# A graph layer's second product: every block decoded from bytes, instead of four kept as ready weights

## The chip, the cores and the metric

The kernel runs on one core of one Trainium2 chip. A core has a matrix engine (TensorE, PE in the profile), a vector engine (VectorE, DVE), an activation engine (ScalarE, ACT), a general engine (GpSimd, POOL) and a sync engine that issues transfers (SyncE, SP). Each takes its own instructions in their order, and they wait for each other through semaphores. The metric is the time of one execution on the device in microseconds: the median of three runs.

## What is computed

Two graph layers over 3327 nodes of 64 features, with one adjacency matrix of 3327 x 3327. The first layer is a sum over pairs of nodes; the second is a product of a weight matrix with the features of all nodes. Cut to what matters:

```python
h = jnp.maximum(_layernorm(x, axis=-1), 0.0)
# layer 0, for all pairs (i, j)
adj_att = sigmoid(left[:, None] + right[None, :] + b_att[0]) * adj
x_local = logmap(x[:, None, :], x[None, :, :], c)
support_t = jnp.einsum('ij,ijd->id', adj_att, x_local)
x = x + proj(expmap(h, support_t, c), c)        # per node, over 64 features
# layer 1
h = jnp.maximum(_layernorm(x, axis=-1), 0.0)
support = h @ weight
mask = (adj != 0)
rank = jnp.cumsum(mask, axis=1)
deg = rank[:, -1:]
k = jnp.minimum(deg, 100.0)
pos = rank - (deg - k)
w = mask * jnp.where(pos > 0, 0.5 ** (k - pos), 0.0)
x = x + w @ support + bias
```

Each edge of the second layer has a weight that halves with every later edge of its row. It needs the same adjacency blocks as the first layer, so the kernel reads them once and keeps one number for each pair.

## The kernel before

The nodes are padded to 26 blocks of 128. The first layer goes over four strips of output nodes (8, 8, 6 and 4 blocks), and in each over the 26 source blocks j, from the last to the first, in rounds. A round loads a piece of the adjacency matrix (`ad`), makes a mask of it, lets PE count the later edges (`pc`), and keeps a byte for each pair (`behind`). Times 128 and read as a bf16 pattern, that number is the weight of the pair in the second layer, because it then stands in the exponent. The rest of a round is a tanh (`sg`), a product (`pq`), two Gelu, two vector instructions, and the product that sums over j (`po`).

```python
JD = range(12, 16)
AHEAD = 2
SGB, ADB = 5, 5
PORTIONS, LAST = (2, 4, 4, 8), 6
...
behind_hi = const.tile([P, NB - JD.stop, NP], U8, name="behind_hi")
weight_of = const.tile([P, len(JD), NP], U16, name="weight_of")
...
def read(n, j):                       # what is kept of a counted block
    kept = behind(j)[:, S.i0 : S.i0 + S.F]
    if (n < AHEAD and k == 0) or i * num // den != (i + 1) * num // den:
        A.activation(kept, S.pc[:, : S.F], AF.Relu, scale=128.0 if j in JD else 1.0)
    elif j in JD:
        V.tensor_scalar(kept, S.pc[:, : S.F], 0.0, 128.0, op0=ALU.max, op1=ALU.mult)
    else:
        V.tensor_scalar(kept, S.pc[:, : S.F], 0.0, None, op0=ALU.max)
```

Blocks 12 to 15 are kept as 16-bit weights (`weight_of`), ready for PE; the other 22 as bytes (`behind_lo`, `behind_hi`), to be decoded later.

When a strip's sums are complete, they are copied out (`strip_out`), transposed (`turn`) and go through the per-node work (`post`): products of 64 features on DVE, and chains of small steps on one number per node. For the first three strips the small steps run on POOL, hidden behind the next strip. For the last strip they run on DVE, with names ending in `_last`, and with each square root as a power on POOL:

```python
def root(y, v):
    power(y, v, nhalf)               # G.tensor_tensor(..., op=ALU.pow)
    mul(rt, y, y)
    ...
def post(agg, k):
    A.activation(u, v, AF.Square)
    V.tensor_mul(w, hs, v)
    ...                              # dots_last, of_sum_last, d_last, e_last, t_last; first root
    A.activation(k_, t0, AF.Tanh)    # k_last
    ...                              # e_last, of_end_last, d_last, y_last; second root
    V.tensor_add(xs, xs, u)
    V.tensor_reduce(t0, xs, AX.X, ALU.add)
    V.scalar_tensor_tensor(w, wide(t0, nb), -1.0 / D, xs, op0=ALU.mult, op1=ALU.add)
    A.activation(u, w, AF.Square)    # u_last<-w_last
    V.tensor_reduce(t0, u, AX.X, ALU.add)
    ...                              # third root
    V.scalar_tensor_tensor(w, w, 0.0, wide(rn, nb), op0=ALU.max, op1=ALU.mult)
    A.copy(s2[:, bs, 0], w)          # the cast
    V.tensor_sub(s2[:, bs, 1], w, s2[:, bs, 0])
```

The work is cut into portions, and `advance(n)` lets some of them into the order of instructions between others. In the second product the decodes alternate between ACT and DVE; each block is then multiplied with the features `s2`, in seven pieces. The four last blocks need the last strip's features and come at the end.

```python
weights = {j: decode(j) for j in order[: len(JD) + 1]}   # order: 12 to 15, then 0 to 11, then 16 to 21
stages.append(Stage(per_node(len(STRIPS) - 1, pa)))
...
def decode(j):
    if j in JD:
        return behind(j)
    wt = l1.tile([P, NP], U16, name="wt", bufs=7)
    decoded += 1
    if decoded % 2:
        A.activation(wt, behind(j), AF.Copy, scale=128.0)
    else:
        V.tensor_scalar(wt, behind(j), 128.0, None, op0=ALU.mult)
    return wt
...
for i, j in enumerate(order):
    if j not in weights:
        weights[j] = decode(j)
    asked_of_act()
    advance(LAST)
    for n in range(len(chunks)):
        add(j, weights[j], n)
finish()
for j in range(late, NB):            # blocks 22 to 25
    weights[j] = decode(j)
```

After that each of the seven pieces gets its last four matmuls, is copied, multiplied with the second layer's weight matrix, added to x and sent out. A check on the range of the values (`in_range`) sets a flag by which a slower general path would be taken; with these inputs it isn't.

Of the kernel before, what the change touches and what calls it, by code (L numbers as in the profile page):

```python
# [22 lines left out]
P = 128  # L23
# [4 lines left out]
K = D + 2  # L28
STRIPS = [(0, 8), (8, 8), (16, 6), (22, 4)]
FMAX = 8 * P  # L30
JD = range(12, 16)
IN_ORDER = {mybir.EngineType.PE, mybir.EngineType.DVE, mybir.EngineType.Activation}
AHEAD = 2
SGB, ADB = 5, 5
ON_ACT = ((1, 2), (5, 8), (3, 4), (1, 2))


PORTIONS, LAST = (2, 4, 4, 8), 6
BIG, LATER, ACT = 4, 99, 100
ROUND = (3.5, 3.5, 2.8, 1.9)  # L40

# [402 lines left out]
def fast(ctx, tc, x, adj_t, r, w_att, b_att, weight, bias, out, flag):  # L444
# [84 lines left out]

    jz = const.tile([P, NB, P], F16, name="jz")  # L530
    ju = const.tile([P, NB, P], F16, name="ju")
    behind_hi = const.tile([P, NB - JD.stop, NP], U8, name="behind_hi")
    weight_of = const.tile([P, len(JD), NP], U16, name="weight_of")
    s2 = const.tile([P, NB, 2, D], F16, name="s2")

    left_d = tc.dram_tile([NP], F32, name="left_d")
# [3 lines left out]
    behind_of = {}  # L540

    def behind(j):
        if j in JD:
            return weight_of[:, j - JD.start]
        return behind_of["lo"][:, j] if j < JD.start else behind_hi[:, j - JD.stop]

# [59 lines left out]
    def load(n):  # L608
        k, lo, hi = rounds[n]
        S = strips[k]  # L610
        ad_of[n] = ad = work.tile([P, FMAX], F32, name="ad", bufs=ADB)
        nc.sync.dma_start(ad[:, : span(n)].rearrange("p (b f) -> p b f", f=S.F),
                          adj_t[lo * P : hi * P, S.i0 : S.i0 + S.F].rearrange("(b p) f -> p b f", p=P))
# [19 lines left out]
    def read(n, j):  # L633
        k, lo, hi = rounds[n]
        S = strips[k]
        kept = behind(j)[:, S.i0 : S.i0 + S.F]
        num, den = ON_ACT[k]
        i = NB - 1 - j
        if (n < AHEAD and k == 0) or i * num // den != (i + 1) * num // den:
            A.activation(kept, S.pc[:, : S.F], AF.Relu, scale=128.0 if j in JD else 1.0)  # L640
        elif j in JD:
            V.tensor_scalar(kept, S.pc[:, : S.F], 0.0, 128.0, op0=ALU.max, op1=ALU.mult)
        else:
            V.tensor_scalar(kept, S.pc[:, : S.F], 0.0, None, op0=ALU.max)  # L644

# [22 lines left out]
                T.matmul(S.po[: D + 1, f0:f1], hw[:, j, :], part(n, sg_of[n], j, f0, f1),  # L668
                         start=j == NB - 1, stop=j == 0)

    sums, pairs = ctx.enter_context(ExitStack()), ctx.enter_context(ExitStack())
    ps = sums.enter_context(tc.tile_pool(name="ps", bufs=1, space=PSUM))
    strip = pairs.enter_context(tc.tile_pool(name="strip", bufs=2))
    work = pairs.enter_context(tc.tile_pool(name="work", bufs=2))
    for n in range(AHEAD + 2):
        load(n)
    pairs.enter_context(tc.manual_schedule(engines=IN_ORDER))

# [159 lines left out]
    def last_of_ahead():  # L838

        p4 = ps.tile([P, 16, P], F16, name="po")  # L840
        turned_to(p4, low, 0)
        kept(p4, low, 0)

        wn, opx = small("wn"), small("opx")
        V.tensor_scalar(wn, nrm, WA / 2, None, op0=ALU.mult)
        V.tensor_scalar(opx, x2, c_c, 1.0, op0=ALU.mult, op1=ALU.add)
        V.tensor_mul(hw[:, :, D], opx, wn)
        V.tensor_mul(wn, wn, y)
        V.tensor_mul(hw[:, 13:, :D], rl[:, 13:], wide(wn[:, 13:], 13))
        yield  # L850
        logits((later,))
        left_to_dram()
        yield
        V.tensor_mul(hw[:, :13, :D], rl[:, :13], wide(wn[:, :13], 13))
        V.tensor_scalar(ih, babs, 2 / WA, None, op0=ALU.mult)
        V.tensor_scalar(balm, bal, MIN_NORM, None, op0=ALU.max)
        V.tensor_mul(su, nrm, balm)
        V.tensor_mul(sv, bal, su)
        V.reciprocal(sk, balm)
        V.tensor_scalar(sk, sk, sqc, None, op0=ALU.mult)  # L860
        V.tensor_scalar(maxnorm, absr, 1.0 - EPS_BALL, None, op0=ALU.mult)
        V.tensor_mul(c2_c, c_c, c_c)
        V.tensor_scalar(m2c, c_c, -2.0, None, op0=ALU.mult)
        V.tensor_scalar(p2c, c_c, 2.0, None, op0=ALU.mult)
        ahead.close()

        behind_of["lo"] = ctx.enter_context(tc.tile_pool(name="lo", bufs=1, side="right", reuse_waits="tile")).tile(
            [P, JD.start, NP], U8, name="behind_lo")
        yield


# [11 lines left out]
        V.tensor_reduce(st[:, 3:4], t1, AX.X, ALU.min)  # L883
        V.tensor_scalar(st[:, 3:4], st[:, 3:4], -1.0, None, op0=ALU.mult)

    def in_range():
        pf = ps.tile([P, P], F32, name="pc")
        T.transpose(pf[:4, :], st, ident)
        st2 = post_pool.tile([4, 1], F32, name="st2")
        V.tensor_reduce(st2, pf[:4, :], AX.X, ALU.max)  # L890
        yield
        pf = ps.tile([P, P], F32, name="pc")
        T.transpose(pf[:1, :4], st2, ident[:4, :4])
        st3 = post_pool.tile([1, 4], F32, name="st3")
        V.tensor_copy(st3, pf[:1, :4])  # L895
        ok = post_pool.tile([1, 2], F32, name="ok")

        V.tensor_mul(ok, st3[:, 0:4:2], st3[:, 1:4:2])
        V.tensor_scalar(ok[:, 0:1], ok[:, 0:1], QMAX / 2, None, op0=ALU.is_le)
        V.tensor_scalar(ok[:, 1:2], ok[:, 1:2], 0.0, None, op0=ALU.is_equal)  # L900
        V.tensor_mul(ok[:, 0:1], ok[:, 0:1], ok[:, 1:2])
        V.tensor_scalar(flag, ok[:, 0:1], -1.0, 1.0, op0=ALU.mult, op1=ALU.add)
        yield


    class Asked:
# [177 lines left out]
    def turn(k):  # L1084
        pa = ps.tile([P, FMAX], F32, name="po")
        for b in range(STRIPS[k][1]):
            c0 = (b // 4) * 512 + (b % 4) * (D + 1)
            T.transpose(pa[:, c0 : c0 + D + 1], strips[k].ot[:, b * P : (b + 1) * P], ident[: D + 1, : D + 1])
        return pa
# [36 lines left out]
        stages.clear()  # L1126

    stages, rest_of_ahead = [Stage(range_steps())], last_of_ahead()
    range_end = in_range()
    for n in range(R):  # L1130
        k, lo, hi = rounds[n]
        m, w = n + AHEAD, span(n)
        ended, turned = (n > i and rounds[n - i - 1][1] == 0 for i in (1, 2))
        if m + 2 < R:
            if rounds[m + 2][2] == NB:
                strip_in(rounds[m + 2][0])
            load(m + 2)
        two = m < R and len(js(m)) == 2
        if two:
            count(m, js(m)[0])  # L1140
# [36 lines left out]
        advance(PORTIONS[k])  # L1177
        if turned:
            total(n - 2)
        if n > R - 3:  # L1180
            next(range_end)
    total(R - 2)
    total(R - 1)
    strip_out(len(STRIPS) - 1)
    pa = turn(len(STRIPS) - 1)
    pairs.close()


    w2s = const.tile([P, D], F32, name="w2s")
    V.tensor_scalar(w2s, w2, 2.0**27 / HS, None, op0=ALU.mult)  # L1190
    late = STRIPS[-1][0]
    order = [*JD, *range(JD.start), *range(JD.stop, late)]
    chunks = halves(NP)
    with tc.tile_pool(name="l1", bufs=2, reuse_waits="tile") as l1, tc.manual_schedule(engines=IN_ORDER):
        decoded = 0

        def decode(j):

            nonlocal decoded
            if j in JD:  # L1200
                return behind(j)
            wt = l1.tile([P, NP], U16, name="wt", bufs=7)
            decoded += 1
            if decoded % 2:
                A.activation(wt, behind(j), AF.Copy, scale=128.0)  # L1205
            else:
                V.tensor_scalar(wt, behind(j), 128.0, None, op0=ALU.mult)  # L1207
            return wt

        weights = {j: decode(j) for j in order[: len(JD) + 1]}  # L1210
        stages.append(Stage(per_node(len(STRIPS) - 1, pa)))
        sums.close()
        l1_ps = ctx.enter_context(tc.tile_pool(name="l1_ps", bufs=1, space=PSUM, reuse_waits="tile"))
        pw = [l1_ps.tile([P, f1 - f0], F32, name=f"pw{n}") for n, (f0, f1) in enumerate(chunks)]

        def add(j, wt, n):
            f0, f1 = chunks[n]
            T.matmul(pw[n], s2[:, j].rearrange("p c d -> p (c d)"), wt[:, f0:f1].bitcast(BF16),  # L1218
                     start=j == order[0], stop=j == NB - 1)

        def bias(b0, nb):
            xb = x_sb[:, b0 : b0 + nb]
            G.tensor_add(xb, xb, bias_b[:, None, :].to_broadcast([P, nb, D]))  # L1223

        for i, j in enumerate(order):
            if j not in weights:
                weights[j] = decode(j)
            asked_of_act()
            advance(LAST)
            for n in range(len(chunks)):  # L1230
                add(j, weights[j], n)
            if i % 4 == 3 and i < STRIPS[-2][0]:
                bias(i - 3, 4)
        finish()
        bias(STRIPS[-2][0], late - STRIPS[-2][0])
        bias(late, NB - late)
        for j in range(late, NB):
            weights[j] = decode(j)
        ow = [l1.tile([P, 512], F32, name="ow", bufs=4)[:, : f1 - f0] for f0, f1 in chunks]

        def close(n):
            f0, f1 = chunks[n]
# [9 lines left out]

        for n in range(len(chunks)):
            for j in range(late, NB):
                add(j, weights[j], n)
            if n % 2:
                A.copy(ow[n], pw[n])
            else:
                V.tensor_copy(ow[n], pw[n])
            if n > 1:  # L1260
                close(n - 2)
# [54 lines left out]
```

## Time and profile before

| | before |
|---|---|
| median of 3 runs | 436.24 us (435.56 to 436.67) |
| span of the profiled run | 434.5 us |
| mean clock granted to PE | 0.967 |
| pairs (first layer) | until about 372 us |
| second product | about 374.6 to 427 us |

In the profile a row of busy tenths cuts the span into 40 equal slices, and each digit is the busy share of an engine in one slice. A row of a timeline gives the start in us, the duration, the engine, the line of the kernel, the operation and its tiles, output before input, with sizes and types; a bracket holds the time that the engine was idle before it, and what it waited for. Two instructions of one engine can overlap a little, so a run of equal ones takes less than the sum of their durations.

The groups that matter for the second product:

```profile
L1205 ACT ACTIVATE wt<-behind_lo x6: 2960/2964/2977, 369.1 to 392.9; 128x3328 uint16<-128x3328 uint8 x6
L1207 DVE TENSOR_SCALAR wt<-behind_lo x6: 1885/1886/1894, 381.2 to 399.1; 128x3328 uint16<-128x3328 uint8 x6
L1205 ACT ACTIVATE wt<-behind_hi x5: 2958/2961/2971, 395.8 to 411.6; 128x3328 uint16<-128x3328 uint8 x5
L1207 DVE TENSOR_SCALAR wt<-behind_hi x5: 1879/1886/1886, 401.5 to 411.1; 128x3328 uint16<-128x3328 uint8 x5
```

The three numbers are the shortest, median and longest duration in ns, then come the first and last start in us. There are 11 decodes on ACT and 11 on DVE.

### The profile page before, as it was taken

Reading aid. Unit: us, or ns where it says so; the run is one execution under the profiler, and the core shown is the slowest. Engines: PE = TensorE matmul, PEld = TensorE weight load, DVE = VectorE, ACT = ScalarE, POOL = GpSimd, SP = SyncE. Lnnn points to the kernel's source line nnn. Section 1 sums busy time; section 2 is a strip of 40 time slices with the busy share of each in tenths; the row PEclk is TensorE's granted clock in tenths of the full one; section 3 lists DMA queues with packets and bytes.
Section 4 is the critical chain, followed back from the end, with each engine's and each line's share of the span. In section 5 each row is a group of like instructions: output and inputs, shape, how many; then the busy total and the mean of one; then the engine's idle time right before and its main releaser. Section 6 shows DMA issues by size and latency. Waiting matters only on the chain.

```text
span 434.5 us, 4704 instructions
## 1 busy us (share of the span) xinstructions
PE 364.4 (84%) x1460; PEld 155.8 (36%) x1460; DVE 377.1 (87%) x556; ACT 365.0 (84%) x409; POOL 111.4 (26%) x218
## 2 busy tenths in 40 slices
PE   0227499999999899999999899999777999877983
PEld 0014233333333333333333454444332333333453
DVE  2776999999999899999999898899988899688931
ACT  3429599999999989999999899999894999399720
POOL 6010000000000035780160083921505183404200
PEclk9999699999999899999999899999996999999987
DMA  8310444545447435543446354444633320000012
GB/s 186 140 38 0 137 147 144 154 151 172 147 150 206 126 122 159 178 148 99 143 121 181 85 148 141 145 129 138 185 106 99 103 90 0 2 0 1 2 25 62
DMA packets 23248, 48.98 MB, mean 113 GB/s; under 512 B 8713, under 2 KB 9169, under 8 KB 23215
## 3 DMA queue, kind: packets, MB, share of 16 engines
q1 hardware_dynamic: 21087, 47.81, 36.6%
q10 hardware_dynamic: 1808, 0.46, 0.6%
q0 software_dynamic: 320, 0.33, 0.5%
q8 instruction: 13, 0.21, 0.2%
q14 instruction: 20, 0.16, 0.1%
HBM read 46.40 MB, written 0.87 MB: 109 GB/s over the span
## 4 chain that ended last, share of the span: by engine, by line
DVE 38%; ACT 23%; PE 22%; issue 10%; POOL 3%; DMA 2%; POOLq 0%; DVEq 0%; ACTq 0%
DVE sg L1173 11%; DVE sg L1154 10%; PE po L668 8%; ACT sg L651 6%; ACT pq L1147 5%; DVE behind_lo L644 3%; ACT pq L1148 3%; PE pc L629 2%; PE pq L658 2%; PE pq L659 2%; PE pc L630 2%; DVE wt L1207 2%; ACT wt L1205 2%; DVE behind_hi L644 2%; ACT behind_lo L640 2%
## 5 line engine op out<-in xcount | busy, mean ns | idle before, releaser
L668 PE MATMUL po<-sg,hw 128*65 128x512 f32 (+1 forms) x364 | 161.1, 566 | 0.4 <-DVE st L895 0.4
L1173 DVE SCALAR_TENSOR_TENSOR sg<-pq,sg 128x1024 f32<-128x1024 f32 (+1 forms) x91 | 103.8, 1140 | 6.6 <-ACT pq L1148 5.3
L1154 DVE SCALAR_TENSOR_TENSOR sg<-sg,ad 128x1024 f32<-128x1024 f32 (+1 forms) x91 | 103.9, 1142 | 2.5 <-ACT sg L651 2.4
L651 ACT ACTIVATE sg<-left_b,right 128x1024 f32<-128x1024 f32 (+2 forms) x103 | 99.5, 978 | 1.0 <-DVE right L819 1.0
L1147 ACT ACTIVATE pq<-pq 128x1024 f32<-128x1024 f32 (+1 forms) x90 | 86.1, 957 | 4.4 <-PE pq L659 4.3
L1148 ACT ACTIVATE pq<-pq 128x1024 f32<-128x1024 f32 (+1 forms) x90 | 85.2, 946 | 2.9
L630 PE MATMUL pc<-mask,cb 128*128 128x512 bf16 (+1 forms) x182 | 66.9, 378 | 16.3 <-DVE mask L618 14.8
L629 PE MATMUL pc<-mask,ca 128*128 128x512 bf16 (+1 forms) x175 | 65.6, 375 | 13.6 <-DVE behind_hi L644 5.8
L668 PEld LDWEIGHTS po<-sg,hw 128*65 128x65 f32 x364 | 49.5, 138 | 70.1 <-issue 55.1
L658 PE MATMUL pq<-iu,ju 71*128 71x512 f16 (+1 forms) x182 | 68.6, 377 | 1.1 <-ACT jz L755 0.4
L659 PE MATMUL pq<-iz,jz 128*128 128x512 f16 (+1 forms) x182 | 67.0, 375 | 0.0
L618 DVE TENSOR_SCALAR mask<-ad 128x1024 bf16<-128x1024 f32 (+1 forms) x91 | 59.0, 649 | 0.0
L630 PEld LDWEIGHTS <-cb 128*128 128x128 bf16 x182 | 18.1, 99 | 69.7 <-issue 52.0
L1218 PE MATMUL pw<-wt,s 128*128 128x512 bf16 (+1 forms) x154 | 33.9, 371 | 7.4 <-DVE wt L1207 5.1
L967 POOL TENSOR_TENSOR dots<-dots,ih 128x8 f32<-128x8 f32 (+1 forms) x3 | 2.6, 876 | 141.1 <-DVE dots L987 141.1
L629 PEld LDWEIGHTS <-ca 128*128 128x128 bf16 x175 | 17.5, 100 | 30.3 <-issue 18.6
L1218 PEld LDWEIGHTS <-s 128*128 128x128 f16 x182 | 18.0, 100 | 26.8 <-issue 9.3
L658 PEld LDWEIGHTS <-ju 71*128 71x128 f16 x182 | 18.2, 100 | 23.9 <-DVE sg L1173 5.2
L640 ACT ACTIVATE behind_hi<-pc 128x1024 uint8<-128x1024 f32 (+2 forms) x24 | 20.7, 864 | 7.1 <-PE pc L630 7.1
L659 PEld LDWEIGHTS <-jz 128*128 128x128 f16 x182 | 18.4, 101 | 19.9 <-issue 3.5
L640 ACT ACTIVATE behind_lo<-pc 128x1024 uint8<-128x1024 f32 (+2 forms) x29 | 24.9, 858 | 0.0
L1223 POOL TENSOR_TENSOR x_sb<-x_sb,bias_b 128x256 f32<-128x256 f32 (+1 forms) x6 | 9.9, 1660 | 49.6 <-DVE w L1056 44.0
(290 smaller groups left out, 364.8 us busy)
## 6 DMA issues: line engine op xcount, KB each, us to landing
ad<-in_adj_t SPq DMA_DIRECT2D x65, 512.0 KB, 3.6
ad<-in_adj_t SPq DMA_DIRECT2D x26, 384.0 KB, 3.1
out<-o SPq DMA_DIRECT2D x6, 128.0 KB, 2.0
left_b<-left_d SPq DMA_DIRECT2D x1, 512.0 KB, 3.3
x_sb<-in_x ACTq DMA_DIRECT2D x1, 416.0 KB, 5.7
x_sb<-in_x SPq DMA_DIRECT2D x1, 416.0 KB, 4.9
iz<-jz SPq DMA_DIRECT2D x3, 128.0 KB, 2.4
left_b<-left_d SPq DMA_DIRECT2D x1, 384.0 KB
```

The costliest lines, as they stand in the source:

```text
L618: V.tensor_scalar(*args, 0.0, None, op0=ALU.not_equal)
L629: T.matmul(S.pc[:, f0:f1], ca, S.before[:, f0:f1], start=False, stop=True, skip_group_check=True)
L630: T.matmul(S.pc[:, f0:f1], cb, now[:, f0:f1], start=S.first, stop=True, skip_group_check=True)
L640: A.activation(kept, S.pc[:, : S.F], AF.Relu, scale=128.0 if j in JD else 1.0)
L651: A.activation(part(n, sg, j), S.left[:, : S.F], AF.Tanh, bias=right[:, j : j + 1], scale=0.5)
L658: T.matmul(part(n, pq, j, f0, f1), ju[:KB, j, :], S.iu[:, f0:f1], start=True, stop=False)
L659: T.matmul(part(n, pq, j, f0, f1), jz[:, j, :], S.iz[:, f0:f1], start=False, stop=True)
L668: T.matmul(S.po[: D + 1, f0:f1], hw[:, j, :], part(n, sg_of[n], j, f0, f1), start=j == NB - 1, stop=j == 0)
L1147: A.activation(pq, pq, AF.Gelu, scale=-WG / QS)
L1148: A.activation(pq, pq, AF.Gelu, scale=WH)
L1154: V.scalar_tensor_tensor(sg, sg, 1.0, ad_of.pop(n)[:, :w], op0=ALU.add, op1=ALU.mult)
L1173: V.scalar_tensor_tensor(sg, pq, WD, sg, op0=ALU.add, op1=ALU.mult)
```

## The change

The change was handed over with the words "fixed order ahead of the pairs, strip sums copied ahead of the second product on two engines, per-node scalars two per instruction with timed slots, in place of: fixed order ahead of the pairs". Most of what these words name stands in both kernels. The kernels differ in this:

- No block is kept as ready 16-bit weights. All 26 are kept as bytes and decoded in the second product, in the order 0 to 25, the even ones on DVE and the odd ones on ACT. This frees memory on the chip (`weight_of`).
- The freed memory goes to two more buffers for adjacency loads (7 for 5), and the loads run three rounds ahead of the first stage that needs them instead of two.
- The last strip's sums are copied (`agg_last`) before the first decode on ACT. Before, the first decode stood ahead of that copy.
- The check on the range moves from the last two rounds of the pairs into the second product, ahead of the matmuls of block 8.
- `LAST`, which says how much per-node work goes between two blocks, is 8 instead of 6.

```diff
-JD = range(12, 16)
+JH = 13
-SGB, ADB = 5, 5
+SGB, ADB = 5, 7
-PORTIONS, LAST = (2, 4, 4, 8), 6
+PORTIONS, LAST = (2, 4, 4, 8), 8
...
-    behind_hi = const.tile([P, NB - JD.stop, NP], U8, name="behind_hi")
-    weight_of = const.tile([P, len(JD), NP], U16, name="weight_of")
+    behind_hi = const.tile([P, NB - JH, NP], U8, name="behind_hi")
...
-            A.activation(kept, S.pc[:, : S.F], AF.Relu, scale=128.0 if j in JD else 1.0)
-        elif j in JD:
-            V.tensor_scalar(kept, S.pc[:, : S.F], 0.0, 128.0, op0=ALU.max, op1=ALU.mult)
+            A.activation(kept, S.pc[:, : S.F], AF.Relu)
...
-    for n in range(AHEAD + 2):
+    for n in range(AHEAD + 3):
         load(n)
...
-        if n > R - 3:
-            next(range_end)
     total(R - 2)
     total(R - 1)
     strip_out(len(STRIPS) - 1)
-    pa = turn(len(STRIPS) - 1)
+    stages.append(Stage(per_node(len(STRIPS) - 1, turn(len(STRIPS) - 1))))
     pairs.close()
...
-            if j in JD:
-                return behind(j)
             wt = l1.tile([P, NP], U16, name="wt", bufs=7)
-            decoded += 1
-            if decoded % 2:
+            if j % 2:
                 A.activation(wt, behind(j), AF.Copy, scale=128.0)
...
-        weights = {j: decode(j) for j in order[: len(JD) + 1]}
-        stages.append(Stage(per_node(len(STRIPS) - 1, pa)))
...
-        for i, j in enumerate(order):
-            if j not in weights:
-                weights[j] = decode(j)
+        for j in range(late):
+            wt = decode(j)
             asked_of_act()
             advance(LAST)
+            if j == 8:
+                in_range(l1_ps)
             for n in range(len(chunks)):
-                add(j, weights[j], n)
+                add(j, wt, n)
```

## The prediction

> **What bounds the kernel now.** I read the page first: engines, then slices.
>
> ```profile
> span 434.5 us, 4704 instructions
> ...
> PE 364.4 (84%) x1460; PEld 155.8 (36%) x1460; DVE 377.1 (87%) x556; ACT 365.0 (84%) x409; POOL 111.4 (26%) x218
> ...
> DVE  2776999999999899999999898899988899688931
> ACT  3429599999999989999999899999894999399720
> ```
>
> Three engines above 84% means no single bound, so a change has to be placed in a stage. Next came the table of stages, which has for each stretch its length, then busy time and count of PE, PEld, DVE, ACT, POOL, then clock and DMA.
>
> ```profile
> 340.00:350.00 10.00, 9.26 (x34) 3.44 (x32) 9.73 (x11) 9.88 (x15) 2.38 (x6) 1.00 0.42 133
> ...
> 370.00:380.00 10.00, 8.78 (x38) 3.54 (x37) 6.43 (x25) 3.12 (x4) 4.22 (x9) 1.00 0.01 2
> 380.00:390.00 10.00, 7.76 (x40) 3.62 (x38) 8.73 (x26) 9.28 (x5) 0.91 (x1) 1.00 0.00 0
> 390.00:400.00 10.00, 8.23 (x41) 3.82 (x40) 8.65 (x20) 9.59 (x6) 3.40 (x2) 1.00 0.00 0
> ...
> 410.00:415.00 5.00, 2.73 (x15) 1.18 (x13) 3.02 (x2) 4.52 (x2) 0.00 (x0) 1.00 0.00 0
> ```
>
> The pairs (to about 372 us) keep PE, DVE and ACT all full. In the second product, which follows, ACT is the full one: 9.3 to 9.6 of 10 us, while PE and DVE have air; at 410 to 415 PE is busy for 2.73 of 5. So I read ACT's order of time there. A row is start, duration, operation, and in brackets the idle time before it.
>
> ```profile
> 369.05 2.97 ACT L1205 ACTIVATE wt<-behind_lo 128x3328 uint16<-128x3328 uint8 x1
> 374.77 0.38 ACT L1098 COPY agg_last<-po 128x260 f32<-128x260 f32 x1 [2.75 <-PE po L1088]
> ...
> 380.05 0.51 ACT L1070 CAST s<-w 128x384 f16<-128x384 f32 x1 [4.17 <-DVE w L1067]
> ...
> 384.31 11.58 ACT L1205 ACTIVATE wt<-behind_lo 128x3328 uint16<-128x3328 uint8 x4
> ...
> 405.50 0.40 ACT L1070 CAST s<-w_last 128x256 f16<-128x256 f32 x1 [3.05 <-DVE w_last L1067]
> 405.81 8.70 ACT L1205 ACTIVATE wt<-behind_hi 128x3328 uint16<-128x3328 uint8 x3
> ```
>
> The decode wt<-behind takes ACT 2.90 us back to back (8.70 / 3). The first stands at 369.05, where ACT would only have waited for the last strip's sums. The last ends at 414.5; PE starts again at 414.57, and 19.9 us later the span ends. That time, **the end of ACT's last decode**, is what I have to move. ACT has idle holes before it (2.75, 4.17 and 3.05 us here, 0.63 at 384.07 and 0.41 at 399.17) because it works in order and must wait for small steps of the per-node work on DVE. Those steps wait for POOL:
>
> ```profile
> 379.50 1.41 POOL L967 TENSOR_TENSOR rn_last<-t_last,nhalf 128x4 f32<-128x4 f32 x1
> 390.96 2.62 POOL L967 TENSOR_TENSOR rn_last<-y_last,nhalf 128x4 f32<-128x4 f32 x1 [10.05 <-DVE y_last L967]
> ...
> 390.82 1.89 DVE L1207 TENSOR_SCALAR wt<-behind_lo 128x3328 uint16<-128x3328 uint8 x1
> ```
>
> The same power of four numbers takes 1.41 us alone, and 2.62 us beside a DVE decode; DVE then waited 0.90 us for it.
>
> **What the Trainium skill says.** "SBUF — State Buffer", section "Who interferes with whom": an instruction of VectorE in a two-port mode holds the port pair that it shares with GpSimd for its whole length, and the other waits. The trace agrees: both powers met by a decode (at 390.96 and 401.63) end 0.87 and 0.88 us after that decode's end. So where a power falls matters. "ScalarE: Activation LUTs", section "What ACT_TABLE_LOAD costs", gives 186 ns + 0.833 ns per element and an overlap of 93 ns back to back; for 3328 elements that is 2.96 us, and the trace has 2.96 to 2.98, spaced 2.90. "TensorE: Matmul & The Clock Gate", section "What's actually happening": an idle window of some 3.4 us halves PE's clock. The trace has 0.50 from 416 to 419, after the pause before 414.57; so the last phase may shift by a microsecond or two either way.
>
> **The change, part by part.**
>
> *Four more decodes.* Before, blocks 12 to 15 were written by the pairs as 16-bit weights already scaled; now every block is a byte and is decoded. 22 decodes (11 on each engine) become 26 (13 and 13): 2 x 2.90 = 5.8 us more on ACT, 2 x 1.80 = 3.6 us on DVE (1.89 each, 1.80 from start to start). In the pairs nothing is saved: the write of a block in the pairs, over its widths, took DVE a median of 1.21 us as weight_of and 1.21 as behind_lo, and ACT 0.80 us as either.
>
> *The hole at 369.05.* In the built order ACT's first decode now stands behind the copy of agg_last and the square u_last, so the idle slot is lost: 2.90 us. By itself, ACT has 3 x 2.90 = 8.7 us more to do after the sums than before. But the early decodes fill the 4.17 us hole at 380.05, and the other holes move. I therefore replayed the tail in the built order, each engine in order, with the durations of the trace.
>
> *The check for range.* Its steps leave the end of the pairs (one of 0.19 us on DVE was in the chain) and go to block 8 of the second product. The last sums then start 0.2 us earlier, at 371.35; with the 1.93 us of products, 0.7 of copy and 0.5 of transposes of the trace, agg_last is copied at 374.55.
>
> *Replay, ACT:* u_last ends 375.3; decodes 1, 3, 5 until 384.0; the cast of strip 2 (0.4); k_last waits for DVE until 385.15; decodes 7, 9, 11, 13 from 385.35 to 397.0; then the square u_last waits for DVE's w_last.
>
> *Replay, DVE:* copy to 374.0; decode 0; sums; decode 2 to 379.2; 1.76 us of small steps to 380.9; decode 4, which meets the first power and puts its end to 383.6; steps to 385.1; decode 6 to 386.9; steps to 389.4; decode 8 to 391.2; y_last at 392.0. No decode follows directly, so this power takes 1.4 and ends at 393.45. The check for range (0.3 with PE's part, then 0.9) runs meanwhile and is done at 393.4, so it costs nothing. Six steps (1.25), w_last, decode 10 to 396.9, four vector steps (1.7), decode 12 to 400.4, w_last at 400.85.
>
> *End of it:* ACT's square starts at 400.85, a hole of 3.85 us. Decode 15 to 404.1. DVE's decode 14, from 401.85 to 403.75, meets the third power: end 404.6. Then 0.8 and 0.45 of steps, and ACT's cast starts at 405.9, a hole of 1.8. Five decodes follow (17 to 25): 406.25 + 5 x 2.90 + 0.06 = **420.8**. As addition: 375.3, 13 x 2.90 = 37.7, small work 1.3, holes 1.1 + 3.85 + 1.8 = 6.75, together 421.0. Before it was 414.5. PE then has one matmul less left than before (0.2 us), since the last decode is now block 25.
>
> The sum: 420.9 - 414.5 - 0.2 = **+6.2 us**, on a median of 436.24: **442.5 us**.
>
> *Seven buffers and loads three rounds ahead.* In the pairs no mask instruction waits for its load (idle 0.0 before 91 of them); loads land 3.5 us after issue. I give it 0.
>
> **Rivals.**
> 1. *Deeper loading helps the pairs.* For it: loads wait 265 us in total for free buffers. Against: nobody waits for the loads; and PE, DVE and ACT are at 9.3 to 9.9 of 10 already. Worth 0, at most -1: 441.5.
> 2. *Seven loads at the start delay it.* DVE stands still until 13.01 for the small weight transfer, with the DMA engines 0.93 to 0.98 busy from 4 to 14 us. Two more loads are 1.05 MB, 2.7 us at the 394 GB/s of 12 to 14. If they shared out time with the earlier ones, the start would slip by up to 2.7: 445. Against: of the five loads the last three landed 11.2, 11.6 and 12.0 us after their issues, which follow each other from 1.29 to 4.28 us, so they landed in their order; the two new ones stand behind, and from 16 to 30 almost nothing moves.
> 3. *ACT's holes all close,* if DVE's small steps come earlier than I replay: then ACT's last decode ends at 421.0 - 6.75 = 414.3 and the kernel stays at 436. Against: the steps are chained and DVE has two decodes more between them, so I don't believe in more than 2 us.
> 4. *The powers all meet decodes* (2.6 instead of 1.4 for the second) or the holes grow: 1.2 to 2.5 us more, 444 to 445.
>
> **Range and chances.** The replay is a sum of measured durations in a known order; its uncertain terms are the two holes of ACT (1.5 each), the clock of PE in the last phase (1.7) and the start (rarely 2.7). That gives 439.5 to 446.0. 2% above the median is 444.96, which needs 2.5 us more than I have: 0.2. For 2% faster there is no mechanism: 0.02.
>
> **What will show it.** The pairs should end within 0.5 us of before (last sg product near 371.3). ACT should have 13 decodes of 2.96 us, the first near 375.3, with a hole of 3 to 5 us before the square u_last near 401 and of about 2 before the cast near 406; the last decode ends near 421. The second power should take about 1.4. PE should restart right after ACT's last decode and the span end some 19.7 us later. I am wrong if the pairs move by more than 2 us, if ACT's holes vanish, or if PE is no longer waiting for ACT at the end.

## The result, and the profile after

| | before | after |
|---|---|---|
| median | 436.23 us (435.56 to 436.67, 4 runs) | 442.59 us (441.13 to 443.27, 4 runs) |
| ratio to before | | 1.0143 (95% interval 1.011 to 1.0175) |
| span of the profiled run | 434.5 us | 441.2 us |
| ACT's last decode ends | 414.51 us | 420.20 us |
| from there to the end of the span | 20.0 us | 21.0 us |

The kernel became 1.4% slower; 442.5 us had been predicted. From the page of the changed kernel:

```profile
span 441.2 us, 4708 instructions
...
PE 366.3 (83%) x1460; PEld 156.2 (35%) x1460; DVE 380.5 (86%) x558; ACT 370.6 (84%) x411; POOL 110.4 (25%) x218
```

ACT has 5.6 us more work than before and DVE 3.4, as four more decodes should cost. The shares stay the same, and say nothing of the 6.4 us. The table of stages, with the same columns as before (length, busy time and count of PE, PEld, DVE, ACT and POOL, clock, DMA):

```profile
340.00:350.00 10.00, 9.26 (x34) 3.46 (x32) 9.73 (x11) 9.88 (x16) 2.40 (x6) 1.00 0.25 80
380.00:390.00 10.00, 8.78 (x43) 3.93 (x41) 8.95 (x31) 9.30 (x6) 3.13 (x4) 1.00 0.00 0
390.00:400.00 10.00, 6.07 (x30) 2.83 (x30) 9.23 (x26) 6.79 (x3) 1.01 (x1) 1.00 0.00 1
410.00:415.00 5.00, 5.00 (x27) 2.38 (x25) 4.76 (x3) 5.00 (x3) 0.00 (x0) 1.00 0.01 3
```

The pairs (340 to 350) are the same to 0.00 us on PE, DVE and ACT. From 390 to 400 ACT now works 6.79 of 10 us where it worked 9.59. From 410 to 415 it is full, because decodes remain. So ACT waits in the middle of the stage and has work left at its end. ACT's own order of time shows both:

```profile
374.60 0.38 ACT L1091 COPY agg_last<-po 128x260 f32<-128x260 f32 x1 [5.05 <-PE po L1081]
375.32 8.69 ACT L1192 ACTIVATE wt<-behind_lo 128x3328 uint16<-128x3328 uint8 x3
383.93 0.50 ACT L1063 CAST s<-w 128x384 f16<-128x384 f32 x1
385.12 0.20 ACT L1002 ACTIVATE k_last<-t_last 128x4 f32<-128x4 f32 x1 [0.70 <-DVE t_last L960]
...
400.42 0.42 ACT L1052 ACTIVATE u_last<-w_last 128x256 f32<-128x256 f32 x1 [3.63 <-DVE w_last L1049]
400.75 2.96 ACT L1192 ACTIVATE wt<-behind_hi 128x3328 uint16<-128x3328 uint8 x1
405.45 0.41 ACT L1063 CAST s<-w_last 128x256 f16<-128x256 f32 x1 [1.74 <-DVE w_last L1060]
405.76 14.44 ACT L1192 ACTIVATE wt<-behind_hi 128x3328 uint16<-128x3328 uint8 x5
```

Compare the last two rows with those of before. The cast of the last strip's features stands at 405.45 here and stood at 405.50 there. Behind it stand five decodes here and three there. So the cast comes no later than before, although four more decodes are done, and two decodes' time is added after it. That the cast stays is owed to `LAST` of 8, which asks for the per-node steps earlier: with 6 it comes later, as a run below shows. POOL's and DVE's rows around the powers:

```profile
380.99 2.60 POOL L960 TENSOR_TENSOR rn_last<-t_last,nhalf 128x4 f32<-128x4 f32 x1 [0.29 <-DVE t_last L960]
392.00 1.01 POOL L960 TENSOR_TENSOR rn_last<-y_last,nhalf 128x4 f32<-128x4 f32 x1 [8.41 <-DVE y_last L960]
401.57 2.59 POOL L960 TENSOR_TENSOR rn_last<-t_last,nhalf 128x4 f32<-128x4 f32 x1 [0.38 <-DVE t_last L960]
```

The first and third power met a decode on DVE (2.60 and 2.59 us); the second had none beside it, and took 1.01.

Last, PE in the end phase, and the clock there (the number ahead of the DMA share in the stage rows):

```profile
417.39 0.59 PE L1199 MATMUL pw<-wt,s 128*128 128x512 bf16 x2 [1.09 <-ACT wt L1192]
420.25 4.00 PE L1199 MATMUL pw<-wt,s 128*128 128x512 bf16 x9 [2.27 <-ACT wt L1192]
```

```profile
416.00:420.00 4.00, 0.89 (x4) 0.21 (x3) 0.00 (x0) 4.00 (x2) 0.00 (x0) 0.91 0.00 0
420.00:424.00 4.00, 3.75 (x9) 1.51 (x9) 0.69 (x1) 0.79 (x2) 0.00 (x0) 0.50 0.00 0
424.00:428.00 4.00, 4.00 (x23) 3.19 (x22) 1.27 (x3) 0.58 (x1) 0.00 (x0) 0.74 0.15 35
```

PE restarts 0.05 us after ACT's last decode, so ACT still sets the end. The clock is 0.50 from about 419.3 to 426.1 (worked out from 0.91, 0.50 and 0.74), for 6.8 us. In before PE's restart and the clock looked like this:

```profile
414.57 3.22 PE L1218 MATMUL pw<-wt,s 128*128 128x512 bf16 x10 [2.27 <-ACT wt L1205]
```

```profile
413.00:416.00 3.00, 1.43 (x7) 0.70 (x7) 0.71 (x2) 1.52 (x1) 0.00 (x0) 0.97 0.00 0
416.00:420.00 4.00, 4.00 (x17) 2.71 (x16) 1.11 (x2) 0.58 (x1) 0.00 (x0) 0.59 0.00 0
```

From 0.97 and 0.59 I work out some 3.4 us of half clock there, and from 420 on it is 1.00. From ACT's last decode to the end the changed kernel thus takes another microsecond, 21.0 us for 20.0.

### The profile page after: what moved, and what is told of

It is laid out like the page before. It is cut to its first block, busy times and chain, and to the rows that moved or that the text cites. A ratio compares the mean times of both kernels' runs of the same rounds, so it can differ in the third digit from the quotient of the medians.

```text
span 441.2 us, 4708 instructions
## 1 busy us (share of the span) xinstructions
PE 366.3 (83%) x1460; PEld 156.2 (35%) x1460; DVE 380.5 (86%) x558; ACT 370.6 (84%) x411; POOL 110.4 (25%) x218
## 4 chain that ended last, share of the span: by engine, by line
DVE 39%; ACT 24%; PE 22%; issue 11%; DMA 2%; POOL 1%; POOLq 0%; DVEq 0%; ACTq 0%
DVE sg L1165 11%; DVE sg L1146 10%; PE po L663 7%; ACT sg L646 6%; ACT pq L1139 5%; ACT wt L1192 3%; DVE behind_lo L639 3%; ACT pq L1140 3%; PE pw L1199 3%; DVE behind_hi L639 3%; PE pc L626 2%; PE pq L653 2%; PE pc L627 2%; PE pq L654 2%; DVE wt L1194 2%
## 5 line engine op out<-in xcount | busy, mean ns | idle before, releaser
L1199 PE MATMUL pw<-wt,s 128*128 128x512 bf16 (+1 forms) x182 | 41.3, 377 | 9.9 <-DVE wt L1194 5.7
L627 PEld LDWEIGHTS <-cb 128*128 128x128 bf16 x182 | 18.1, 99 | 69.6 <-issue 51.9
L637 ACT ACTIVATE behind_hi<-pc 128x1024 uint8<-128x1024 f32 (+2 forms) x30 | 26.0, 866 | 9.6 <-PE pc L627 9.6
L637 ACT ACTIVATE behind_lo<-pc 128x1024 uint8<-128x1024 f32 (+2 forms) x32 | 27.3, 852 | 0.0
L639 DVE TENSOR_SCALAR behind_hi<-pc 128x1024 uint8<-128x1024 f32 (+2 forms) x22 | 22.0, 999 | 3.4 <-PE pc L627 3.4
```

Source lines behind the costliest of these rows:

```text
L627: T.matmul(S.pc[:, f0:f1], cb, now[:, f0:f1], start=S.first, stop=True, skip_group_check=True)
```

## The experiments

Two theories of the 6 us were set against each other.

- **A:** the end is the time of the cast, plus 0.3, plus 2.90 us for each ACT decode that stands *behind* the cast, plus the end phase of PE. Decodes elsewhere are hidden in ACT's holes.
- **B:** every decode on ACT, and every idle slot lost, adds its 2.90 us to the end, wherever it stands.

The pairs are the same in the variants of the changed kernel, but end up to 1.7 us apart from run to run (the copy of agg_last between 374.60 and 376.27). I therefore read the stretch from that copy to the cast, and not the absolute times. The variants were timed in three groups, in which before had 436.72, 436.75 and 437.14 us; the ratios are to the before of the same group, and times of different groups compare only to about 1 us. Half clock is counted while PE still has products to do.

| kernel | copy to cast, us | ACT decodes behind the cast | ACT's last decode to the end, us | half clock in it, us | time, us | ratio (interval) |
|---|---|---|---|---|---|---|
| before | 30.73 | 3 | 20.0 | 3.4 | 436.23 | 1 |
| after | 30.85 | 5 | 21.0 | 5.9 | 442.59 | 1.0143 (1.011 to 1.0175) |
| loads back | 30.85 | 5 | 21.1 | 6.0 | 443.75 | 1.0154 (1.012 to 1.0189) |
| first decode ahead | 30.71 | 5 | 19.6 | 3.4 | 442.14 | 1.0132 (1.01 to 1.0164) |
| ACT one decode ahead | 31.16 | 4 | 17.6 | 0 | 438.31 | 1.0036 (1.0024 to 1.0048) |
| last decode on DVE | 30.85 | 4 | 18.7 | 0 | 438.73 | 1.0046 (1.0033 to 1.0059) |
| before, no ready weights | 33.80 | 3 | 20.2 | 3.4 | 439.86 | 1.0069 (1.0046 to 1.0092) |
| after, portions of six | 35.16 | 3 | 17.8 | 0 | 439.58 | 1.0065 (1.0041 to 1.0089) |
| extra decode in the hole | 30.84 | 5 | 21.0 | 6.0 | 443.70 | 1.0147 (1.0114 to 1.0179) |
| extra decode behind the cast | 30.85 | 6 | 19.3 | 3.3 | 445.77 | 1.0204 (1.0176 to 1.0233) |
| PE kept busy | 30.86 | 5 | 18.1 | 0 | 440.59 | 1.0089 (1.0062 to 1.0117) |
| placed, on before | 30.69 | 1 | 19.0 | 0 | 430.03 | 0.984 (0.9819 to 0.9861) |
| placed, on after | 33.94 | 1 | 19.0 | 0 | 433.18 | 0.9908 (0.9883 to 0.9933) |

### Are the deeper loads worth anything?

```diff
-SGB, ADB = 5, 7
+SGB, ADB = 5, 5
-    for n in range(AHEAD + 3):
+    for n in range(AHEAD + 2):
-        if m + 3 < R: ... load(m + 3)
+        if m + 2 < R: ... load(m + 2)
```

> The changed kernel, but with five load buffers and loads two rounds ahead, as before. Theory (the added time is in the second product, and nobody waits for the loads): the time of the changed kernel, 442.6 us within 1, and the last product of the pairs starts within 0.2 us of 370.1. Rival (the deeper loads help or hurt the pairs by about 1 us or more): the pairs end later or earlier by that, 441.5 or 443.6 us.

443.75 us against 442.59, with intervals that lie on each other. The stretch from the copy to the cast is 30.85 us in both. The pairs ended 0.5 us later than in the changed kernel, outside the 0.2 that I had allowed, but within the 1.7 by which they vary with the deeper loads in place. Neither help nor harm of the loads is seen beyond that scatter. This answers rivals 1 and 2 of the prediction as far as the scatter allows, and the start didn't slip either: DVE's wait for the small weight transfer ended at 13.01 us in before, at 12.86 in the changed kernel and at 13.14 here.

### Is the lost idle slot at 369 us a cost?

```diff
+        weights = {1: decode(1)}          # ahead of the copy of agg_last on ACT
         stages.append(Stage(per_node(len(STRIPS) - 1, pa)))
...
         for j in range(late):
-            wt = decode(j)
+            if j not in weights:
+                weights[j] = decode(j)
+            wt = weights[j]
```

> The changed kernel, but ACT's first decode (block 1) stands ahead of the copy of the last strip's sums again, in the idle time near 369 us; the other decodes stay where they are between the per-node steps. Theory A (ACT's end is set by the time of the cast of the last strip's features, near 405.5 us, and by the number of decodes that stand behind it, five): nothing is gained, 442.6 us within 1; the holes before the cast grow by 2.9 us together. Rival B (the idle slot lost at 369 costs its 2.9 us, as my addition put it): 439.7 us, last decode of ACT ends near 417.3.

ACT's order of time in this run:

```profile
369.35 2.97 ACT L1189 ACTIVATE wt<-behind_lo 128x3328 uint16<-128x3328 uint8 x1
...
383.51 0.51 ACT L1063 CAST s<-w 128x384 f16<-128x384 f32 x1 [1.77 <-DVE w L1060]
385.26 0.20 ACT L1002 ACTIVATE k_last<-t_last 128x4 f32<-128x4 f32 x1 [1.24 <-DVE t_last L960]
...
405.62 0.40 ACT L1063 CAST s<-w_last 128x256 f16<-128x256 f32 x1 [1.75 <-DVE w_last L1060]
405.93 14.44 ACT L1189 ACTIVATE wt<-behind_hi 128x3328 uint16<-128x3328 uint8 x5
```

The slot is used again, and most of the 2.90 us come back as holes: 1.77 us before the cast of strip 2, and 1.24 instead of 0.70 before k_last, where ACT waits for DVE. The same five decodes stand behind the cast. The time is 442.14 us, the same within the interval. The slot by itself gains nothing that can be seen, and theory B, which gives it 2.90 us, falls here.

### One decode fewer behind the cast, in two ways

```diff
         for j in range(late):             # ACT one decode ahead
-            wt = decode(j)
+            if j % 2:
+                weights[j + 2] = decode(j + 2)
+            else:
+                weights[j] = decode(j)
+            wt = weights[j]
```

> As the run before, and ACT decodes one block of its own further ahead all through, so that four instead of five decodes stand behind the cast. Theory A: ACT's last decode ends 2.3 to 2.9 us earlier, near 417.5 us of the span, and the time is 440.2 us (439.5 to 441). Rival B (sum of ACT's work, wherever it stands): 439.7 us, the same as the run before. Rival C (PE or the vector engine sets the end): 442.6 us.

```diff
-            if j % 2:                     # last decode on DVE
+            if j % 2 and j != NB - 1:
                 A.activation(wt, behind(j), AF.Copy, scale=128.0)
```

> The changed kernel, but the last block (25) is decoded by DVE instead of ACT: four decodes of ACT and six of DVE behind the cast. Theory A: ACT's last decode ends near 417.3 and DVE's near 416.6, PE has less idle time, 439.8 us (438 to 440.5). Rival C (ACT isn't what the end waits for): 442.6 us.

The first keeps all 13 decodes on ACT and moves each one place forward (with the slot at 369 us and an eighth buffer). The second takes one decode from ACT. Both leave four behind the cast, and both come to the same time: 438.31 and 438.73 us. So it counts where a decode stands, not how many ACT has. But they gained 4.3 and 3.9 us by the medians, where one decode is 2.90; the first came out below the 439.5 to 441 that I had expected. The rest is in the end phase: no half clock there, and 17.6 and 18.7 us from ACT's last decode to the end instead of 21.0. I had not reckoned with that second term, and the experiment on PE's clock below takes it up.

### Which part of the change costs the time?

```diff
-JD = range(12, 16)                        # before, no ready weights; the tile weight_of goes too
+JD = range(13, 13)
```

> The kernel before with one part of the change alone: no ready weights, all 26 blocks decoded; the first decode of ACT ahead of the sums' copy, portions of 6, five load buffers, and the range check in the pairs stay. In its order three decodes of ACT stand behind the cast of the last strip, as in the kernel before, but two more DVE decodes stand ahead of the steps that lead to the cast. Theory A (the cast's time and the decodes behind it): the cast comes 3 us later, near 408.5, ACT's last decode ends near 417.5, and the time is 439.6 us (438.5 to 440.7). Rival B (ACT's added work of 5.8 us counts wherever it stands): 442 us.

```diff
-PORTIONS, LAST = (2, 4, 4, 8), 8          # after, portions of six; nothing else
+PORTIONS, LAST = (2, 4, 4, 8), 6
```

> The changed kernel with portions of 6 instead of 8. In its order three decodes of ACT stand behind the cast instead of five, while the cast comes later, because one more DVE decode stands ahead of it and the range check no longer runs beside a power. Theory A: cast near 409 to 410, plus 0.3 and three times 2.90, so ACT's last decode ends near 418.5, and the time is 441 us (439.5 to 442). Rival B (ACT's work wherever it stands): no change, 442.6 us.

ACT at the end of the stage, first in before without the ready weights, then in after with portions of six:

```profile
409.16 0.41 ACT L1069 CAST s<-w_last 128x256 f16<-128x256 f32 x1 [3.05 <-DVE w_last L1066]
409.47 8.70 ACT L1204 ACTIVATE wt<-behind_hi 128x3328 uint16<-128x3328 uint8 x3
```

```profile
410.39 0.39 ACT L1063 CAST s<-w_last 128x256 f16<-128x256 f32 x1
410.69 8.71 ACT L1192 ACTIVATE wt<-behind_hi 128x3328 uint16<-128x3328 uint8 x3
```

Without the ready weights the cast comes 3.1 us later, counted from the copy (33.80 for 30.73), with three decodes behind it as before, and the time goes up by 3.1 us. Two more decodes on ACT ahead of the cast are 5.8 us of work; 3.1 of them show, and the rest fell into holes. Portions of six on the changed kernel put the cast 4.3 us later (35.16 for 30.85), and take away two decodes behind it (5.8). Together that should save 1.5 us, and ACT's last decode does end 1.4 us sooner after the copy (44.17 for 45.60). The time fell by 3.0, to 439.58 (3.4 by the ratios); I had expected 441. Again most of the difference lies in the clock: 17.8 us from the last decode to the end instead of 21.0.

So the ratio of 1.0143 has two parts of about equal size. Decoding all blocks, with portions of six, gives 1.0065 (the changed kernel) or 1.0069 (before); the rest, some 3 us, comes with `LAST` of 8. It brings the cast forward by 4.3 us, leaves 5.8 us of decodes over behind it, and loses more in PE's clock.

### The same extra work in two places

```diff
             wt = decode(j)
+            if j == 13:                   # in the hole; 21 for behind the cast
+                A.activation(l1.tile([P, NP], U16, name="extra", bufs=1), behind(j), AF.Copy, scale=128.0)
             asked_of_act()
```

Nobody reads the extra decode.

> The changed kernel with one more decode on ACT, whose result nobody reads, straight ahead of the last square u_last, where ACT stood idle for 3.63 us. Theory A (only the decodes that stand behind the cast of the last strip's features count): the hole shrinks to about 0.7 us, the cast stays at 405.5 and the time at 442.6, within 1 us. Theory B (every decode on ACT adds its 2.90 us to the end, wherever it stands): 445.5.

> The changed kernel with the same unused decode on ACT, now behind the cast of the last strip's features, so that six stand there and not five. Theories A and B both: ACT's last decode ends 2.90 us later, near 423.1, and the time is 445.5; with PE's longer wait the clock may take up to 1.7 more. If the time stayed at 442.6, something other than ACT's decodes would set the end.

ACT with the extra decode in the hole, then with it behind the cast:

```profile
397.38 2.96 ACT L1209 ACTIVATE extra<-behind_hi 128x3328 uint16<-128x3328 uint8 x1
401.10 0.42 ACT L1052 ACTIVATE u_last<-w_last 128x256 f32<-128x256 f32 x1 [0.76 <-DVE w_last L1049]
401.42 2.96 ACT L1192 ACTIVATE wt<-behind_hi 128x3328 uint16<-128x3328 uint8 x1
406.13 0.41 ACT L1063 CAST s<-w_last 128x256 f16<-128x256 f32 x1 [1.74 <-DVE w_last L1060]
406.44 14.44 ACT L1192 ACTIVATE wt<-behind_hi 128x3328 uint16<-128x3328 uint8 x5
```

```profile
407.12 0.40 ACT L1063 CAST s<-w_last 128x256 f16<-128x256 f32 x1 [1.75 <-DVE w_last L1060]
407.43 8.71 ACT L1192 ACTIVATE wt<-behind_hi 128x3328 uint16<-128x3328 uint8 x3
416.05 2.96 ACT L1209 ACTIVATE extra<-behind_hi 128x3328 uint16<-128x3328 uint8 x1
418.91 5.83 ACT L1192 ACTIVATE wt<-behind_hi 128x3328 uint16<-128x3328 uint8 x2
```

In the hole it shrinks the wait from 3.63 to 0.76 us; the cast, counted from the copy, doesn't move (30.84 us), and the ratio is 1.0147 for 1.0143. Behind the cast it puts ACT's last decode to 17.62 us after the cast instead of 14.75, and the ratio to 1.0204. So ACT's last decode ends 2.87 us later, for one decode of 2.90; ahead of the cast it doesn't move. This is theory A with one instruction in two places. The time is not so clean a measure: it rises by 2.7 us by the ratios to before, and by 2.1 against the run with the decode in the hole, because the end phase shrank from 21.0 us to 19.3. More of the half clock (421.2 to 428.1, worked out in the same way) fell ahead of ACT's last decode here.

### Is the rest the clock of PE?

```diff
             for j in range(late, NB):
+                if n == 0 and j % 2:      # products nobody reads, in PE's two last waits
+                    for _ in range(16 if j == late + 1 else 36):
+                        T.matmul(warm, s2[:, 0]..., weights[0][:, :128].bitcast(BF16), start=True, stop=True)
                 add(j, weights[j - late], n)
```

> The changed kernel with 52 small products on PE, whose result nobody reads, in its two last waits for ACT (16 ahead of the products of block 23, 36 ahead of those of block 25), so that PE does not stand idle there. ACT's last decode should still end near 420.2. If the half clock of 419.58 to 426.40 comes of those waits, the clock stays at 1.00, the end phase shrinks from 20.95 us to 19.3 to 19.8, and the time is 441 to 441.5. If the clock falls for another reason, the half clock stays and the time is 442.6 or a little more.

PE around ACT's last decode in this run, then the clock:

```profile
416.32 1.06 PE L1239 MATMUL pf<-wt,s 128*128 128x128 bf16 x16
417.57 0.59 PE L1199 MATMUL pw<-wt,s 128*128 128x512 bf16 x2 [0.19 <-ACT wt L1192]
418.00 2.17 PE L1239 MATMUL pf<-wt,s 128*128 128x128 bf16 x36
420.44 2.10 PE L1199 MATMUL pw<-wt,s 128*128 128x512 bf16 x8 [0.27 <-ACT wt L1192]
```

```profile
416.00:420.00 4.00, 3.81 (x57) 3.31 (x56) 0.00 (x0) 4.00 (x2) 0.00 (x0) 1.00 0.00 0
420.00:424.00 4.00, 3.68 (x24) 2.29 (x22) 1.81 (x3) 0.98 (x2) 0.00 (x0) 1.00 0.00 0
```

ACT's last decode ends as before at 420.39, but the clock stays at 1.00, and the span ends 18.1 us after that decode instead of 21.0. PE has 52 products more to do and the kernel is 2.0 us faster by the median (440.59 for 442.59), more than I had expected. The intervals of the two ratios still touch (1.011 to 1.0175, 1.0062 to 1.0117); against the run with the extra decode in the hole, of the same group, the gain is 3.1 us, and the mean clock is 0.967 to 0.973 in the four executions here, for 0.963 to 0.967 in those of the changed kernel. The half clock comes of PE's waits, and costs the changed kernel 2 to 3 us.

### A version that beats both

If A holds, the decodes should be placed by hand: as many as ACT can do in its holes ahead of the cast, and one behind it. The same instructions are issued in another order, once with the ready weights of before (22 decodes) and once without (26); the second also has eight buffers for decoded blocks and the range check back in the pairs; the comment in the diff explains the names of the steps.

```diff
-        for i, j in enumerate(order):
-            if j not in weights:
-                weights[j] = decode(j)
-            asked_of_act()
-            advance(LAST)
+        # D2: decode of block 2 on DVE; A4: of block 4 on ACT; P15: products of block 15; the rest: per-node steps
+        for step in ("D1", "P12", "A_u", "A3", "t_u", "P13", "D2", "P14", "A_ulast", "w_last",
+            "dots1", "A4", "dots2", "P15", "smallA", ...
+            "D21", "A22", "P19", "P20", "smallF", "wl4", "D23", "A_castlate", "P21", "A24",
+            "s2late", "D25"):
```

> The kernel before, with its ready weights, but with every decode of the second product placed by hand: one or two of ACT's in each of its holes, one behind the cast; DVE's moved so that the steps to the cast come earlier or run beside a power; 11 decodes on each. Theory A: cast near 404.5, ACT's last decode ends near 407.5, PE never waits for a decode and is the bound of the second product; its last four blocks begin near 406 instead of 414, and the time is 430.5 us (429 to 432.5), 1.0 to 1.6% below the kernel before. Rival B (ACT's 11 decodes and their sum set the end): 436 us.

> The changed kernel (no ready weights, seven load buffers), with the 26 decodes placed in the same way, 13 on ACT and 13 on DVE, and the range check back in the pairs. Theory A: one decode of ACT behind the cast, cast near 408.5, last decodes near 411.5, 433.6 us (432 to 436), below the kernel before although it decodes four blocks more. Rival B (26 decodes cost 5.8 us more than 22): 442 us.

ACT and PE in the version with ready weights:

```profile
406.07 0.41 ACT L1072 CAST s<-w_last 128x256 f16<-128x256 f32 x1 [0.70 <-DVE w_last L1069]
406.38 2.97 ACT L1201 ACTIVATE wt<-behind_hi 128x3328 uint16<-128x3328 uint8 x1
```

```profile
380.80 18.42 PE L1207 MATMUL pw<-wt,s 128*128 128x512 bf16 x90
...
410.03 2.10 PE L1207 MATMUL pw<-wt,s 128*128 128x512 bf16 x9 [0.25 <-DVE wt L1203]
```

With 22 decodes it takes 430.03 us, 1.6% less than before: the cast is as early (30.69 us after the copy), one decode stands behind it instead of three, PE runs through 90 products from 380.80 without a wait and keeps its clock. I had expected the cast a microsecond earlier; it isn't. With all 26 decodes it takes 433.18, which is some 2% below the changed kernel. There the cast is 3.2 us later, with four decodes more ahead of it, two each on ACT and DVE. In both, PE's last wait is for a decode of DVE (0.25 and 1.19 us), no longer for one of ACT. So the ready weights are worth about 3 us in either order (3.15 here, 3.1 above), and the order of the decodes more than that (6.7 us on before).

## Why the prediction was right

**The pairs.** ACT's copy of agg_last was put at 374.55 and came at 374.60. The loads were given 0, and the run with the loads put back agrees.

**The replay.** ACT's decodes were to start at 375.3 (375.32), k_last at 385.15 (385.12), the square of u_last at 400.85 after a hole of 3.85 (400.42, 3.63), the cast at 405.9 after 1.8 (405.45, 1.74), and the last decode to end at 420.8 (420.20). The 0.45 us of difference at the cast are one term: the second power, taken as 1.4 us, the duration of before's lone one, took 1.01. That one had not been quite alone: DVE's `w<-w,rn` (379.45, 0.56 us) ran beside it.

**The check on the range** was to be hidden beside that power. It nearly was: the power ended at 393.01, DVE's last step of the check at 393.28, and DVE's next small step started at 393.21. It costs at most 0.2 us.

**The end phase** was taken as 19.7 us. It took 21.0, because the half clock of PE lasted 6.8 us (5.9 of them in the end phase) instead of 3.4. The prediction had named the clock as worth a microsecond or two either way, but left it out of the sum. This is the term that was mis-sized, and it made up for the decode that ended 0.6 us too early: by spans, 5.7 + 1.0 us against the +6.2 predicted. The mechanism was right; that the total came within 0.1 us of the measured median is luck.

**"The idle slot is lost: 2.90 us"** was a step that doesn't stand. As bookkeeping it was harmless, since the sum came from the replay. But the run with the slot put back shows no gain from the slot alone. What cost the time is that two more decodes are left over behind the cast, which itself stays where it was, and the longer half clock. The replay had the five decodes behind the cast in its order, but the prediction named neither that count nor `LAST` as a cause.

**The rivals.** Of the first two nothing was seen. The third, that ACT's holes all close, didn't happen: 3.63 and 1.74 us stayed open, because DVE's chain of steps, with two decodes more in it, sets when they end. The fourth was the wrong way round: the second power met no decode.

## What to carry to other kernels

Where an engine that works in order sets the end of a stage, look for the point at which the stage's last input passes through it, here the cast. Count the long instructions behind that point: each puts the end of the engine's work back by its whole length, while the same instruction ahead of it may cost nothing, as the extra decode showed (0 and 2.87 us for one instruction of 2.96). And when the engine at the end waits, ask what the wait does to its clock: here 52 products that nobody reads saved 2 to 3 us.

## What the hardware showed that I had not expected

**PE's clock and short waits.** The Trainium skill, "TensorE: Matmul & The Clock Gate", section "What's actually happening", has free-running windows of some 3.4 us, and half clock after an idle one. The lengths agree: each whole stretch of half clock in the second product, while PE still had products to do, was 3.4 or 6.8 us long. I take the 3.4 us ahead of each fall of the clock as a window. Then no window was wholly idle here. In before, PE waited 2.27 us, the window held 1.3 us of work, and half clock followed. In after, the window up to 419.3 had some 2.4 us of waiting and 1.0 of work, and the next one, in which PE waited 1.0 us more, was followed by half clock too. Waits of 1.1 us and less, alone, had none behind them ("last decode on DVE", "ACT one decode ahead"), nor did the one of 2.10 us in "portions of six". In the middle of the stage PE has another wait, for DVE's step of the range check, of 2.12 to 2.16 us in eight of the kernels. It was followed by 3.4 us of half clock in "loads back", "last decode on DVE" and both runs with an extra decode, and by none in the changed kernel, "first decode ahead", "ACT one decode ahead" and "PE kept busy". And in "extra decode in the hole" the clock fell at 392.7 and at 420.1 us, which is 8.0 times 3.4 apart. That a wait counts by how it falls across fixed windows fits all of these; no edit here tested it.

**POOL and DVE.** By the Trainium skill, "SBUF — State Buffer", section "Who interferes with whom", when DVE's instruction is in a two-port mode, the one of the two that comes first holds the shared ports for its whole instruction, and the other blocks. No run here shows the mode of a decode itself. Decodes that started first did hold the powers back: 2.6 us beside one decode, 3.56 beside two that follow each other (in "placed, on before"), 1.01 alone. But in the changed kernel a power on 128x6 came 0.55 us ahead of a decode, and it was the power that was held back. POOL, then DVE:

```profile
376.78 2.48 POOL L960 TENSOR_TENSOR rn<-t,nhalf 128x6 f32<-128x6 f32 x1
```

```profile
377.33 1.88 DVE L1194 TENSOR_SCALAR wt<-behind_lo 128x3328 uint16<-128x3328 uint8 x1
```

The decode took its usual 1.88 us and ended at 379.21; the power ended at 379.26. The same power took 1.34 us in before and in "placed, on before", where no decode met it, and 2.48 again in each of the eight variants that keep the changed kernel's order of these two. So on this pair of operations, being first did not protect POOL. Whether that is so for other operations, no run here shows.
